# A four-layer graph network on one core: layers 1 and 2 with plain fp32 matmuls, layer norms by statistics instructions and ACT, and the last attention in an order written out by hand

## The chip, the core and the metric

The kernel runs on one core of one Trainium2 chip. A core has five engines, each with its own queue of instructions that it works off in order: PE (TensorE, matmuls; its weight loads are listed as PEld), DVE (VectorE), ACT (ScalarE), POOL (GpSimd, which also issues the indirect DMAs, the gathers) and SP (SyncE, which issues the plain DMAs). They wait for one another through semaphores only. SBUF is the working memory, 128 partitions wide; PSUM takes the matmul results. The metric is the device time of one execution in microseconds (us), the median of several. A profile is one execution recorded by the hardware.

## What is computed

There are 8 batches (B), 2048 nodes (N) and 64 features (D). The graph `adj` is symmetric, has every node's own edge, and about nine neighbours a node. Each layer's output is added to x and layer-normed:

```python
x = _layernorm(x + _L0_gnn_ref(x, adj, ...))   # attention from two scores per node, over neighbours
x = _layernorm(x + _L1_gnn_ref(x, ..., adj))   # per feature: softmax over neighbours of softplus(x*w0+b0)*wa + ba
x = _layernorm(x + _L2_gnn_ref(x, adj, ...))   # relu(x@W_self + b_self + mean over neighbours of x @ W_neigh + b_neigh), own layer norm
x = _layernorm(x + _L3_gnn_ref(x, adj, ...))   # four heads of dot-product attention, Wo, then a second attention on h2:

scores = jnp.einsum('...nd,...md->...nm', h, h)
scores = jnp.where(mask, scores, NEG)
attn = jax.nn.softmax(scores, axis=-1)
return jnp.einsum('...nm,...md->...nd', attn, h) + b
# out2 = _gat_layer(h2, mask, bo);  z2 = leaky_relu(out2, 0.2);  layer norm of z2 with gamma, beta
```

Layers 1 and 2 need sums over all neighbours, for which the kernel multiplies with the whole 2048 x 2048 edge matrix. Layer 0 and the two attentions of layer 3 work on lists of edges.

## The kernel before

**Tiling.** The nodes are cut into NT = 16 tiles of 128 (P), one node a partition; a tile of features is 128 x (8 x 64) = 128 x 512. `X` holds all 16 tiles in SBUF through all layers. The first stage turns `adj` into `ET` (the edge matrix transposed, fp8, 0 or 1), into lists `src` of neighbours, and into 0/1 selections `SelT` and `Sel` that spread node values to edges and add edge values up to nodes. A node tile's edges fill 3 x 4 blocks of 128 edges (GS = 3 steps s, NG = 4 groups g of 32 nodes), and each block's neighbour rows are fetched by one gather on POOL (`gather`, L164).

**Order.** A scheduler orders the instructions of each engine by program order, priorities and free buffers, except inside the four heads of layer 3, where the order of PE, ACT, DVE and POOL is the program's own (`tc.manual_schedule`). Pools (`bufs=n`) hand out n buffers per name in turn; a buffer is written again only when its last reader is done. Pools of a finished stage give their memory to the next stage's.

**Layer norm** (L123 to L141, helper `layer_norm`) takes a group of tiles ("chunks"). Per tile: sum on DVE (L129), times 1/64 (L130), subtraction (L131), square on ACT (L133), sum on DVE (L134); then once per group `inv_sqrt` (L117 to L121, a starting value and three Newton steps, ten short DVE operations), and per tile the multiplication on DVE (L138), and gamma and beta on POOL (L140, L141) where there are any. Layers 0, 1 and 2 norm in groups of four tiles, the second attention tile by tile.

**Layer 1** (L389 to L447). For each tile t it makes R: y = X*w0+b0 (DVE), softplus by Abs, Exp and Ln on ACT, e = y*wa (DVE), r = exp(e) (ACT) and r*y (DVE). Exp and Ln need different tables on ACT, so that tables are loaded in between. The fp32 r is then split into three bf16 pieces whose sum is r: ACT casts (L426, L428), DVE subtracts (L427), POOL makes the last (L429). The matmuls (L436) run over 16 row tiles `it`, 16 tiles jt, three pieces q and two halves h: 1536 matmuls of 128x128 fp8 weights with 512 bf16 columns. DVE divides (L441, L442) and POOL adds to X (L444).

**Layer 2** (L451 to L504). Per tile: transpose X (L107, L108), one fp32 matmul set with W_self and W_neigh (L479), S = own part (L481), and the neighbour part split into three bf16 pieces of Y (L486 to L489). Then 768 matmuls (L494) of ET with Y, scaling and relu (L497, L498), and per four tiles a layer norm of S with gamma and beta, X += S (L503), a layer norm of X.

**Layer 3, heads** (L524 to L740). POOL copies X to a table in memory (`xtab`, L529); 192 gathers of its rows, four heads' scores and sums; `through_wo` adds the heads up to h2 and writes it to `htab` (SP). This part, up to about 2204 us, is PE's.

**Layer 3, second attention** (L741 to L792, scheduler's order). Per tile it loads hi (its own rows of htab) and converts SelT and Sel; then six units (s, pair of groups), each: two gathers of htab rows into hs (POOL), two matmuls pe = selection x hi (L767), pr = pe*hs and its sum sc (DVE, L770, L773), w = exp(sc+shift) (ACT, L775), pr = hs*w (POOL, L776), and per group the matmuls that add pr into po (L780) and w into pd (L782). After the six units: 1/pd, z = po/pd (L784, L786), + bo (L787), leaky relu (L788), layer norm with gamma and beta, + X (L790), layer norm, store (L792).

Of the kernel before, what the change touches and what calls it, by code (L numbers as in the profile page):

```python
# [21 lines left out]
F32 = mybir.dt.float32  # L22
# [26 lines left out]
def kernel(ctx: ExitStack, tc: tile.TileContext, ins: dict, out: bass.AP):  # L49
# [42 lines left out]
    def along(v):  # L92

        return v.unsqueeze(len(v.shape)).to_broadcast([*v.shape, D])
# [27 lines left out]

    def layer_norm(chunks, pool, gamma=None, beta=None):  # L123

        shape = list(chunks[0].shape)
        n = len(chunks)
        mu, var, rstd, tmp = (small.tile([P, n, B], F32, name=f"ln_{k}{n}") for k in "mvrt")
        for c, v in enumerate(chunks):
            nc.vector.tensor_reduce(mu[:, c], v, AX.X, ALU.add)  # L129
            nc.vector.tensor_scalar_mul(mu[:, c], mu[:, c], 1.0 / D)  # L130
            nc.vector.tensor_tensor(v, v, along(mu[:, c]), ALU.subtract)  # L131
            sq = pool.tile(shape, F32, name="sq")
            nc.scalar.activation(sq, v, AF.Square)  # L133
            nc.vector.tensor_reduce(var[:, c], sq, AX.X, ALU.add)  # L134
        nc.vector.tensor_scalar(var, var, 1.0 / D, EPS, op0=ALU.mult, op1=ALU.add)
        inv_sqrt(rstd, var, tmp)
        for c, v in enumerate(chunks):
            nc.vector.tensor_tensor(v, v, along(rstd[:, c]), ALU.mult)  # L138
            if gamma is not None:
                nc.gpsimd.tensor_tensor(v, v, over(gamma, shape), ALU.mult)  # L140
                nc.gpsimd.tensor_tensor(v, v, over(beta, shape), ALU.add)  # L141
# [3 lines left out]
    ET = main.tile([P, NT, N], FP8, name="ET")  # L145
# [14 lines left out]
    for g in range(NG):  # L160
        nc.vector.memset(group[g * GN:(g + 1) * GN, g:g + 1], 1.0)

# [218 lines left out]

# [5 lines left out]
    with ExitStack() as l1:  # L389
        wp = l1.enter_context(tc.tile_pool(name="l1w", bufs=1))  # L390
        wk = l1.enter_context(tc.tile_pool(name="l1k", bufs=2))
        pa = l1.enter_context(tc.tile_pool(name="l1pa", bufs=6, space=PSUM))
# [16 lines left out]
        R = wp.tile([P, NT, 3, 2, 2, HB * D], BF16, name="R")  # L409
        for t in range(NT):  # L410
# [7 lines left out]
            nc.vector.scalar_tensor_tensor(y, y, 0.0, e, op0=ALU.max, op1=ALU.add)  # L418
            nc.vector.tensor_tensor(e.rearrange("p (b d) -> p b d", d=D), y.rearrange("p (b d) -> p b d", d=D),
                                    over(wa, [P, B, D]), ALU.mult)  # L420
            r = wk.tile([P, 2, 2, HB * D], F32, name="r")
            nc.scalar.activation(r[:, :, 0], e.rearrange("p (h n) -> p h n", h=2), AF.Exp)
            nc.vector.tensor_tensor(r[:, :, 1], y.rearrange("p (h n) -> p h n", h=2), r[:, :, 0], ALU.mult)
            rf = r.rearrange("p h a n -> p (h a n)")
            pieces = [R[:, t, q].rearrange("p h a n -> p (h a n)") for q in range(3)]
            nc.scalar.copy(pieces[0], rf)  # L426
            nc.vector.tensor_tensor(rf, rf, pieces[0], ALU.subtract)  # L427
            nc.scalar.copy(pieces[1], rf)  # L428
            nc.gpsimd.tensor_tensor(pieces[2], rf, pieces[1], ALU.subtract)  # L429

        for it in range(NT):
            po = [pa.tile([P, 2, HB * D], F32, name="pa") for _ in range(2)]
            for jt in range(NT):
                for q in range(3):
                    for h in range(2):
                        nc.tensor.matmul(po[h].rearrange("p a f -> p (a f)"), ET[:, jt, it * P:(it + 1) * P],  # L436
                                         R[:, jt, q, h].rearrange("p a f -> p (a f)"),
                                         start=(jt == 0 and q == 0), stop=(jt == NT - 1 and q == 2))
# [921 lines left out]
```

## Time and profile before

| | us |
|---|---|
| three runs | 2860.0, 2861.23, 2864.49; median 2861.23 |
| the profiled execution's own time | 2860.0 |
| its span, first to last instruction | 2858.1 |
| mean granted TensorE clock, 1 being full | 0.795 |

| engine | busy us | share of the span | instructions |
|---|---|---|---|
| PE | 2117.8 | 74% | 11631 |
| DVE | 1642.5 | 57% | 2924 |
| POOL | 1254.1 | 44% | 1015 |
| ACT | 754.7 | 26% | 1180 |

The chain of work that ended last gives PE 41% of the span, POOL 25%, DVE 13%, time with no visible cause ("issue") 12%. The stages in time: the graph and layer 0's preparation to about 240 us, layer 0 to 624, layer 1 to 1009, layer 2 to 1223 and its last norms to about 1250, tables and weights of layer 3 to 1304, heads to 2204, the second attention from 2232. An fp32 matmul stands in the records as two instructions, so that L620's 768 matmuls are 1536 records. An engine that idles while another one sets the pace costs nothing; what a stage waits for last is what counts.

### The profile page before, as it was taken

Reading aid. Unit: us, or ns where it says so; the run is one execution under the profiler, and the core shown is the slowest. Engines: PE = TensorE matmul, PEld = TensorE weight load, DVE = VectorE, ACT = ScalarE, POOL = GpSimd, SP = SyncE. Lnnn points to the kernel's source line nnn. Section 1 sums busy time; section 2 is a strip of 40 time slices with the busy share of each in tenths; the row PEclk is TensorE's granted clock in tenths of the full one; section 3 lists DMA queues with packets and bytes.
Section 4 is the critical chain, followed back from the end, with each engine's and each line's share of the span. In section 5 each row is a group of like instructions: output and inputs, shape, how many; then the busy total and the mean of one; then the engine's idle time right before and its main releaser. Section 6 shows DMA issues by size and latency. Waiting matters only on the chain.

```text
span 2858.1 us, 31030 instructions
## 1 busy us (share of the span) xinstructions
PE 2117.8 (74%) x11631; PEld 1217.2 (43%) x11678; DVE 1642.5 (57%) x2924; ACT 754.7 (26%) x1180; POOL 1254.1 (44%) x1015
## 2 busy tenths in 40 slices
PE   2363333327899989928999999999999678766662
PEld 2362111102344464416777777777777111111110
DVE  7974465655633355764344444444443487888877
ACT  4541111028200040104344444444443111110100
POOL 0037888843200032453223333333231687777773
PEclk9985555559999999959999999999999555555555
DMA  7214544520000000022222221222120334333330
GB/s 206 89 37 129 141 131 139 142 63 1 0 1 0 1 3 1 1 82 77 60 60 74 64 63 60 75 64 65 58 67 27 112 107 114 104 94 98 96 92 16
DMA packets 101264, 200.89 MB, mean 70 GB/s; under 512 B 51953, under 2 KB 51953, under 8 KB 99057
## 3 DMA queue, kind: packets, MB, share of 16 engines
q0 software_dynamic: 46080, 151.82, 18.5%
q1 hardware_dynamic: 38384, 42.79, 4.6%
q10 hardware_dynamic: 16640, 4.20, 0.7%
q8 instruction: 95, 1.56, 0.2%
q14 instruction: 65, 0.52, 0.1%
HBM read 181.91 MB, written 16.84 MB: 70 GB/s over the span
## 4 chain that ended last, share of the span: by engine, by line
PE 41%; POOL 25%; DVE 13%; issue 12%; ACT 4%; DMA 2%; ACTq 1%; SPq 0%; another core or an unknown queue 0%; POOLq 0%; DVEq 0%
PE pscore L620 12%; POOL hs L164 12%; PE pa L436 9%; PE po L640 6%; POOL pr L776 6%; PE pt L612 4%; POOL hs L362 2%; PE pm L666 2%; PE pm L652 2%; PE pm L657 2%; PE pm L598 2%; DVE tops L206 1%; DMA hs<-htab,src 1%; DVE key L195 1%; DVE hs L362 1%
## 5 line engine op out<-in xcount | busy, mean ns | idle before, releaser
L627 DVE SCALAR_TENSOR_TENSOR w<-w,Sel 128x1024 f32<-128x1024 f32 x192 | 235.4, 1226 | 495.8 <-ACT w L624 495.8
L164 POOL DMA_INDIRECT hs<-htab,src x384 | 409.8, 1067 | 113.7 <-issue 80.2
L164 POOL DMA_INDIRECT xs<-xtab,src x192 | 232.6, 1211 | 398.2 <-PE po L640 374.4
L620 PE MATMUL pscore<-U,xsT 128*128 128x256 f32 x1536 | 376.8, 390 | 19.0 <-ACT U L600 19.0
L436 PE MATMUL pa<-R,ET 128*128 128x512 bf16 x1505 | 339.6, 383 | 53.5 <-ACT R L426 30.5
L620 PEld LDWEIGHTS pscore<-U,xsT 128*128 128x128 f32 x1536 | 286.2, 197 | 56.6 <-ACT U L600 23.4
L767 PE MATMUL pe<-hi,selTf 32*128 32x512 f32 x384 | 227.6, 1122 | 50.5 <-DVE pr L770 45.1
L436 PEld LDWEIGHTS <-ET 128*128 128x128 fp8e4 x1536 | 151.1, 99 | 243.2 <-issue 43.3
L624 ACT ACTIVATE w<-pscore 128x1024 f32<-128x1024 f32 x192 | 196.8, 1025 | 187.1 <-PE pscore L620 184.2
L776 POOL TENSOR_TENSOR pr<-hs,w 128x1024 f32<-128x1024 f32 x96 | 187.1, 1949 | 89.4 <-ACT w L775 88.2
L640 PE MATMUL po<-w,xs 128*64 128x128 f32 x3072 | 213.3, 282 | 1.6 <-DVE w L627 1.6
L640 PEld LDWEIGHTS po<-w,xs 128*64 128x64 f32 x3072 | 166.0, 138 | 109.1 <-issue 58.7
L672 POOL TENSOR_TENSOR h<-h,h2h 128x512 f32<-128x512 f32 x48 | 61.0, 1270 | 261.8 <-DVE h2h L668 252.6
L614 ACT COPY xsT<-pt 128x512 f32<-128x512 f32 x192 | 112.6, 586 | 203.7 <-PE pt L612 199.7
L494 PE MATMUL pa<-Y,ET 128*128 128x512 bf16 x752 | 165.1, 379 | 0.8
L770 DVE TENSOR_TENSOR pr<-pe,hs 128x1024 f32<-128x1024 f32 x96 | 116.7, 1219 | 81.5 <-issue 69.8
L352 PE MATMUL pe<-s1g,selTf 128*128 128x32 f32 x96 | 23.2, 400 | 162.2 <-DVE w L354 113.9
L441 DVE RECIPROCAL rec<-pa 128x256 f32<-128x256 f32 x32 | 53.9, 1726 | 144.9 <-PE pa L436 144.3
L133 ACT ACTIVATE sq<-X 128x512 f32<-128x512 f32 x48 | 30.2, 629 | 401.6 <-DVE X L131 377.1
L767 PEld LDWEIGHTS pe<-hi,selTf 32*128 32x128 f32 x384 | 55.9, 302 | 186.6 <-DVE pr L770 69.0
L612 PE MATMUL pt<-ident,xs 128*128 128x128 f32 x768 | 131.5, 295 | 1.6 <-DMA xs<-xtab,src 1.5
L444 POOL TENSOR_TENSOR X<-X,rec 128x256 f32<-128x256 f32 x32 | 22.5, 726 | 239.9 <-DVE rec L442 239.9
(524 smaller groups left out, 3498.5 us busy)
## 6 DMA issues: line engine op xcount, KB each, us to landing
at<-in_adj SPq DMA_DIRECT2D x16, 1024.0 KB
hs<-htab,src POOLq DMA_INDIRECT x384
htab<-H SPq DMA_DIRECT2D x16, 260.0 KB
X<-in_x ACTq DMA_DIRECT2D x16, 256.0 KB
xtab<-Xo SPq DMA_DIRECT2D x16, 256.0 KB
xi<-xtab SPq DMA_DIRECT2D x16, 256.0 KB
htab<-h SPq DMA_DIRECT2D x16, 256.0 KB
hi<-htab SPq DMA_DIRECT2D x16, 256.0 KB
```

Of the source, the lines that this page charges most:

```text
L164: nc.gpsimd.indirect_dma_start(out=dst, out_offset=None, in_=table[:, :], in_offset=bass.IndirectOffsetOnAxis(ap=src[:, it, s, g:g + 1], a ...
L436: nc.tensor.matmul(po[h].rearrange("p a f -> p (a f)"), ET[:, jt, it * P:(it + 1) * P], R[:, jt, q, h].rearrange("p a f -> p (a f)"), star ...
L494: nc.tensor.matmul(po, ET[:, jt, it * P:(it + 1) * P], Y[:, jt, k], start=(jt == 0 and k == 0), stop=(jt == NT - 1 and k == 2))
L612: nc.tensor.transpose(pt[:, p], xss[k][:, p * P:(p + 1) * P], ident)
L614: nc.scalar.copy(xsTs[k], pt)
L620: nc.tensor.matmul(pscore[:, p], xsTs[k][:, p], Us[it % 2][:, p, :, :, g * GN:(g + 1) * GN].rearrange("p k h i -> p (k h) i"), start=True, ...
L624: nc.scalar.activation(w.rearrange("p a h i -> p (a h i)"), pscore.rearrange("p a h i -> p (a h i)"), AF.Exp)
L627: nc.vector.scalar_tensor_tensor(w3, w3, 3.0e38, edge, op0=ALU.min, op1=ALU.mult)
L640: nc.tensor.matmul(po[half, p], xss[k][:, f0:f0 + D], ws[k][:, p, k_ * HN:(k_ + 1) * HN], start=(s == 0 and p == 0), stop=(s == GS - 1 and ...
L767: nc.tensor.matmul(pe[:, k].rearrange("p b d -> p (b d)"), selTf[nodes, s * P:(s + 1) * P], hi[nodes, :], start=True, stop=True)
L770: nc.vector.tensor_tensor(pr.rearrange("p k b d -> p (k b d)"), pe.rearrange("p k b d -> p (k b d)"), hs.rearrange("p k b d -> p (k b d)") ...
L776: nc.gpsimd.tensor_tensor(pr.rearrange("p k b d -> p (k b) d"), hs.rearrange("p k b d -> p (k b) d"), along(w.rearrange("p k b -> p (k b)" ...
```

## The change

Four things are changed together; the parts of the file that serve other graphs are untouched.

- **Layers 1 and 2 in fp32.** R and Y are kept in fp32, without pieces. For each row tile, `edges` converts a column block of ET (128 x 2048) to fp32 on DVE, and the matmuls use it: 512 in layer 1 and 256 in layer 2, each with fp32 weights and 512 fp32 columns. In layer 1 the halves h come one after the other, with four PSUM buffers for six; wa and the product with r move from DVE to POOL.
- **Layer norm** by `bn_stats`: on pairs of batches with features outermost, so that even and odd elements of one instruction are two batches. Mean and variance come from its output; ACT then applies scale and bias, one operation per batch (8 a tile). gamma and beta stay on POOL. Layer 2's gamma, beta and addition now alternate tile by tile.
- **ET's memory** is given back after layer 2.
- **Second attention.** The heads write h2 + bo to a second table, `ktab`, from which the second attention gathers (hi still comes from htab), so that bo is not added later. Its order is written out: unit u+4's gathers, unit u+1's score, unit u+2's pe matmuls, unit u's multiplication (every third on DVE, the rest on POOL) and sums, and the work after a tile spread over the next tile's units.

```diff
+    def norm_stats(chunks):
+        n = len(chunks)
+        st = small.tile([P, n, NP, 6], F32, name=f"st{n}")
+        for c, v in enumerate(chunks):
+            for a in range(NP):
+                nc.vector.bn_stats(st[:, c, a], v[:, 2 * a:2 * a + 2, :].rearrange("p b d -> p d b"))
+        triples = st.rearrange("p n a (k m) -> p (n a k) m", m=3)
+        var, rstd, tmp, nmr = (small.tile([P, n * B], F32, name=f"ln_{k}{n}") for k in "vrtm")
+        nc.vector.tensor_scalar(var, triples[:, :, 2], 1.0 / D, EPS, op0=ALU.mult, op1=ALU.add)
+        inv_sqrt(rstd, var, tmp)
+        nc.vector.scalar_tensor_tensor(nmr, triples[:, :, 1], -1.0, rstd, op0=ALU.mult, op1=ALU.mult)
+        return rstd, nmr
+    def normed(chunks, stats):
...
+                nc.scalar.activation(v[:, b], v[:, b], AF.Identity, scale=rstd[:, k:k + 1], bias=nmr[:, k:k + 1])
...
+    def edges(dst, it):
+        nc.vector.tensor_copy(dst, ET[:, :, it * P:(it + 1) * P])
...
-        R = wp.tile([P, NT, 3, 2, 2, HB * D], BF16, name="R")
+        R = wp.tile([P, NT, 2, 2, HB * D], F32, name="R")
...
-            nc.scalar.copy(pieces[0], rf)
-            nc.vector.tensor_tensor(rf, rf, pieces[0], ALU.subtract)
-            nc.scalar.copy(pieces[1], rf)
-            nc.gpsimd.tensor_tensor(pieces[2], rf, pieces[1], ALU.subtract)
+            nc.gpsimd.tensor_tensor(s, f.rearrange("p h (b d) -> p (h b) d", d=D), over(wa, s.shape), ALU.mult)
+            nc.scalar.activation(R[:, t, :, 0], s.rearrange("p (h b) d -> p h (b d)", h=2), AF.Exp)
+            nc.gpsimd.tensor_tensor(R[:, t, :, 1], f, R[:, t, :, 0], ALU.mult)
         for it in range(NT):
-            po = [pa.tile([P, 2, HB * D], F32, name="pa") for _ in range(2)]
-            for jt in range(NT):
-                for q in range(3):
-                    for h in range(2):
-                        nc.tensor.matmul(po[h].rearrange("p a f -> p (a f)"), ET[:, jt, it * P:(it + 1) * P],
...
+            A = wk.tile([P, NT, P], F32, name="A")
+            edges(A, it)
             for h in range(2):
+                po = pa.tile([P, 2, HB * D], F32, name="pa")
+                pof = po.rearrange("p a f -> p (a f)")
+                for jt in range(NT):
+                    nc.tensor.matmul(pof, A[:, jt], R[:, jt, h].rearrange("p a f -> p (a f)"),
...
+                nc.scalar.copy(Y[:, t, g * 2 * P:(g + 1) * 2 * P].rearrange("p (q n) -> p q n", q=2), py[:, :, 1])
...
+                nc.tensor.matmul(po, A[:, jt], Y[:, jt], start=(jt == 0), stop=(jt == NT - 1))
...
+                    hb = wk.tile([P, B, D], F32, name="hb")
+                    nc.gpsimd.tensor_tensor(hb, h2s[it], over(bo, hb.shape), ALU.add)
+                    nc.sync.dma_start(ktab[it * P:(it + 1) * P, :], hb.rearrange("p b d -> p (b d)"))
...
+            def weigh(u):
+                eng = nc.vector if u % 3 == 1 else nc.gpsimd
+                wxs[u] = fk.tile([P, 2, B, D], F32, name="wx", bufs=3)
+                eng.tensor_tensor(wxs[u].rearrange("p k b d -> p (k b) d"), hss[u].rearrange("p k b d -> p (k b) d"),
+                                  along(ws[u].rearrange("p k b -> p (k b)")), ALU.mult)
+            def add_up(u):
...
+                for k in range(2):
+                    nodes = slice((g + k) * GN, (g + k + 1) * GN)
+                    nc.tensor.matmul(po[nodes], self_[:, s, nodes], wxs[u][:, k].rearrange("p b d -> p (b d)"),
+                                     start=(s == 0), stop=(s == GS - 1))
+                    nc.tensor.matmul(pd[nodes], self_[:, s, nodes], ws[u][:, k], start=(s == 0), stop=(s == GS - 1))
...
+            after = {1: divide, 2: norm, 3: residual, 5: norm, 6: store}
+            PER = GS * NG // 2
+            AHEAD = 4
+            with tc.manual_schedule(engines=engines):
+                for u in range(AHEAD):
+                    fetch(u)
+                expand(0)
+                expand(1)
+                score(0)
+                for u in range(len(units) + PER):
+                    if u + AHEAD < len(units):
+                        fetch(u + AHEAD)
+                    if u + 1 < len(units):
+                        score(u + 1)
+                    if u + 2 < len(units):
+                        expand(u + 2)
+                    if u < len(units):
+                        weigh(u)
+                        add_up(u)
+                    for j, f in after.items():
+                        it, r = divmod(u - j + 1, PER)
+                        if r == 0 and 1 <= it <= NT:
+                            f(it - 1)
```

`fetch`, `score` and `expand` hold the gathers, L770 to L775 and L767 of before; `residual` holds gamma, beta and + X.

## The prediction

> **What bounds the kernel now.** I read the page first (busy shares, slices, costliest groups), then the chain of waits, then the busy time of each engine in stretches that I cut at the first and last start of each stage's main matmul, then the timeline at the seams. The stages follow one another, each with its own limit, so one share for the whole span says little. In the table by stretches the columns are stretch, length, then busy us (x instructions) of PE, PEld, DVE, ACT, POOL, then the granted TensorE clock.
>
> ```profile
> 240.00:624.00 384.00, 130.03 (x564) 51.63 (x564) 200.74 (x286) 37.84 (x75) 308.49 (x224) 0.54 0.49 134
> 624.00:738.00 114.00, 70.26 (x277) 28.72 (x284) 63.61 (x99) 89.15 (x115) 33.70 (x16) 0.89 0.00 1
> 738.00:1009.00 271.00, 269.34 (x1229) 122.41 (x1252) 104.27 (x165) 9.45 (x15) 21.35 (x31) 1.00 0.00 1
> 1009.00:1057.00 48.00, 39.55 (x192) 33.12 (x193) 34.89 (x87) 29.60 (x77) 21.10 (x32) 0.93 0.02 5
> 1057.00:1223.00 166.00, 165.16 (x754) 75.12 (x768) 108.08 (x226) 18.25 (x31) 51.44 (x40) 1.00 0.00 1
> 1304.00:2204.00 900.00, 879.58 (x6628) 693.33 (x6628) 385.95 (x450) 386.32 (x520) 280.22 (x227) 0.98 0.21 62
> 2232.00:2520.00 288.00, 222.16 (x604) 48.22 (x608) 217.90 (x303) 29.56 (x77) 228.62 (x177) 0.51 0.40 115
> 2520.00:2800.00 280.00, 182.84 (x522) 40.35 (x516) 230.18 (x349) 28.91 (x71) 198.87 (x148) 0.51 0.30 89
> ```
>
> Layer 0 (240 to 624) is POOL's: 308 of 384 us, and 0.30 us of unlabelled gap behind each of its 192 gathers. Layer 1's and layer 2's matmuls (738 to 1009, 1057 to 1223) and the four heads (1304 to 2204) are PE's, at over 97%. From 624 to 738 ACT leads, preparing R. The second attention, from 2232, is nobody's alone: POOL, DVE and PE are each 65 to 82% busy and the clock is 0.51. Its groups (operation, shapes, count, busy us and mean ns, idle before):
>
> ```profile
> L164 POOL DMA_INDIRECT hs<-htab,src x192 | 195.9, 1020 | 57.0 <-issue 30.7 <-POOL pr L776 20.7 <-DMA htab<-h 4.6
> L776 POOL TENSOR_TENSOR pr<-hs,w 128x1024 f32<-128x1024 f32 x96 | 187.1, 1949 | 89.4 <-ACT w L775 88.2
> L770 DVE TENSOR_TENSOR pr<-pe,hs 128x1024 f32<-128x1024 f32 x96 | 116.7, 1219 | 81.5 <-issue 69.8 <-PE po L780 11.2
> L121 DVE SCALAR_TENSOR_TENSOR ln_r<-ln_t,ln_r 128x8 f32<-128x8 f32 x96 | 45.1, 480 | 0.6
> L787 DVE TENSOR_TENSOR z<-z,bo 128x512 f32<-128x512 f32 x16 | 27.9, 1745 | 0.2
> ```
>
> The reader should see that POOL is owed 195.9+57.0+187.1+62.3 (three residual operations a tile) = 502 us of the 564 us from the first L776 (2248.0) to the end of the last (2812.1), the rest being waits for w; and that an 8-element DVE operation takes 480 ns on average although the same line takes about 170 when nothing else runs.
>
> **What the Trainium skill says.** "FP8 and Floating Point Precision", TensorE Precision Notes: true fp32 takes four passes. The trace agrees: the 64 fp32 matmuls L657 stand as 128 records of 616 ns, against 379 ns for a one-pass bf16 record of the same 512 columns; 237 ns more is one more pass, so two passes a record. "TensorE: Matmul & The Clock Gate", Part 1: the clock is at half rate until the array is busy; here 1.00 in layers 1 and 2, 0.51 in the second attention even at 77% busy. "GPSIMD Engine Reference", Key points: POOL shares its SBUF interfaces with those VectorE instructions that have two SBUF inputs or run in a 2-port mode. The trace agrees: L121 lasts 1.91 us beside a POOL multiply of 1.90. For ACT, "ScalarE: Activation LUTs", What ACT_TABLE_LOAD costs, charges 93 ns per pointer operand; L309, with two, takes 810 ns against 620 for L415 without, as stated. No page prices bn_stats.
>
> **The change part by part**, against the profiled execution's own 2860.0 us (span 2858.1; the median of three runs, 2861.23, is 1.2 above).
>
> 1. Layer 1's and 2's matmuls. Forty-nine bf16 records end 10.74 us after the first starts: (10.74-0.379)/48 = 0.216 us each. So before: 1536 x 0.216 = 331 us and 768 x 0.216 = 166 us. Eight fp32 records of 256 columns take 1.89 us: (1.89-0.379)/7 = 0.216, two passes of 256; hence 0.43 per 512-column record, 0.86 per matmul. A weight load (190 ns) hides behind 430. After: 512 x 0.86 = 440 and 256 x 0.86 = 220.
>
> 2. How much of layer 1 hides under the preparation of R. Before, PE starts at 638.7 and a pair of node tiles takes ACT 12.8 us. After, per pair, ACT loses four casts (about 1.0 us each) but the built order holds four table loads instead of two: 4 x 1.29 + 2 x (0.57+0.57+0.67+0.58) = 9.9, taken as 10.1. Layer 0's last norm now puts 32 ACT operations of about 0.36 us (384 fixed plus 64 elements, less the overlap) = 11.4 us between the first two tiles' Exp and Ln: I walk R(0) to 643 and the last R to 715, 20 us earlier than 735. But PE's order is fixed: until the last R arrives it has issued 37 matmuls, the two groups of the first row tile and a few of the next, so 475 x 0.86 = 408 us remain, plus 3 for buffers: end at 1126, not 1009. Cost +117 (110 to 126).
>
> 3. Preparation of Y. The removed casts and subtractions lay beside PE, busy 39.6 of 48 us; they give 3 us. Layer 1's last norm: stats 6 us, then 32 ACT operations, 11.4 us, which stand in ACT's queue before all but two of the copies that PE waits for; before, DVE's part delayed one tile. Cost +8 (4 to 14). Layer 2 itself +54. edges(), 2048 elements on DVE (L195, as long, takes 2.3 us), is written one tile ahead, under 13.8 us of matmuls and in layer 1 under 27.5; without that cover it would cost up to 2.3 us on each of 32 tiles. What it cannot hide is one wait when the first two A are given back, in the 3 us of part 2.
>
> 4. Layer 2 to 3. The last group's two norms: stats 2.3+2.7, first normed chunk 2.9, twelve POOL operations 16.5, then POOL's 16 table copies, the first 12 beside the second norm: about 48 us to the last table write against 56. -8 (-18 to +3). ET's freed memory frees nothing sooner, since POOL's copies queue behind the last addition anyway.
>
> 5. Layer 0. Per tile DVE loses two two-input operations (1.4 us) that made POOL wait, and the bn_stats that replace them have one input. If all came back, 22 us; I take -12 (-25 to 0).
>
> 6. Heads: one POOL add (1.3 us) and a table write per tile where POOL is 31% busy: hidden but for the last, +1. The adds and writes stand before the next gathers on POOL and before the next xtab read on SP, both several steps ahead of need; if that lead were gone they would cost 16 x 1.3. They take the place of L787 (1.7 us on DVE). bo's load moves from the second attention's start to the heads' and is waited for only there.
>
> 7. Second attention, per tile of six units. POOL: 12 gathers (195.9+57.0)/16 = 15.8, four multiplies 7.8, three residual operations 3.9: 27.5 us. DVE: six scores 6 x 2.26, two multiplies 2.3, divide 1.5, two norms of 4 bn_stats plus 12 short operations. bn_stats is not in this trace. From reduce (1.21 us for 1024 elements, 0.68 for 512) 128 would last 0.28 us, and the next starts 0.09 earlier: 0.2 is the low end, since every element is read once at least; if it reads twice, 0.45. I take 0.2 (0.45 would cost 2 us of DVE a tile, of which part comes out in the wait below): norm 0.8+2.4. Sum 24, with waits for POOL's multiplies 27. PE at half clock: 2.0 for pe, 1.85 for po, 0.2 for pd, six times: 24.4. So POOL sets it, but in order: the residual waits for norm (DVE) and 8 ACT operations (2.9 us). DVE may start that unit's score only 4.5 us after the multiply of two units before, since PE's expand stands behind the previous add_up; then score, multiply, norm (7 us) and ACT (3.2) end near 15 us of POOL's cycle, and POOL is there at 12. What queues behind it: gathers and the next multiply, for which PE waits. 27.5+3 = 30.5 us a tile (28 to 34) against 35.3. 16 x 30.5 = 488 against 564: -76. Fill -2. Drain: 46 us from the last multiply to the end becomes PE 2.2, divide 1.9, norm 3.5, ACT 3, POOL 4, norm 3.5, ACT 3, store about 3: 24 to 25, -21.
>
> Sum: -12+117+8+54-8+1-76-2-21 = +61, so 2921 us.
>
> **Rivals.** (a) PE takes over the second attention: the new order puts pd between the two po of a unit. Before, the two po stand together and four records end in 1.92 us, overlapped. If pd breaks that, a unit is 5.76 us at clock 0.51, 34.6 a tile: 2921+66 = 2987. For it: strict order in the program. Against: in layer 0 eight po records of four column groups end in 1.93 us, so a group does not wait for another's queue; and a fully busy PE might get its full clock. (b) Faster, one mechanism: fewer two-input DVE operations, so POOL no longer waits at the shared interface, in layer 0 (all 25) and in the second attention, where gathers run at their undisturbed 1.25 and multiplies at 1.90: 15+7.6+3.8 = 26.4 us a tile and no wait for the norm. 2921-13-66 = 2842. It decides only below some 27 us a tile. Against: 24 short two-input operations a tile remain. (c) The fixed order does not do what it says: stalls trade places, 35.3 us a tile remain: 2998.
>
> **How the numbers follow.** Forecast 0.70 (about 2862 to 2975), (a) 0.13, (b) 0.11, (c) 0.06. 0.2% (5.7 us) is about what a measurement of this kernel can tell from no change. The range 2862 to 2988 takes in the forecast's own unknowns and (a) up to its value, and leaves out (b) and (c), 0.17. Of the forecast, 0.05 falls within 0.2%: faster 0.11, same 0.05, slower 0.84.
>
> **What would show it.** fp32 records spaced 0.43 us at clock 1.00, with layer 1's last near 1126 less layer 0's gain; ACT's 32 norm operations in a row near 626 and after layer 1; heads starting about 160 us later; six units every 30.5 us with POOL's waits in front of the residual; some 25 us after the last multiply. Wrong if PE issues more of layer 1 during R, if a unit of PE takes 5.8 us, if bn_stats is far from 0.2 us, or if POOL shows no waits.

## The result, and the profile after

The changed kernel takes 2958.82 us (median of four runs, 2956.77 to 2964.96) against 2860.61 for the kernel before in the same comparison: 1.0345 times as long, 95% interval 1.0326 to 1.0363. So the change costs about 98 us where 61 were forecast: the direction and the range were right, the size was 37 us short. Its profiled execution has a span of 2958.0 us, 99.9 longer than that of before.

The first view is the busy time of each engine by stretches, cut at the seams of the changed kernel: the columns are stretch, length, then busy us (x instructions) of PE, PEld, DVE, ACT, POOL, the granted TensorE clock, the DMA share and GB/s.

```profile
240.00:635.00 395.00, 127.35 (x564) 51.66 (x564) 177.36 (x275) 59.10 (x154) 309.25 (x224) 0.54 0.47 130
635.00:741.00 106.00, 51.50 (x77) 19.42 (x78) 29.98 (x50) 89.41 (x129) 40.78 (x32) 0.72 0.00 0
741.00:1148.00 407.00, 406.88 (x949) 179.80 (x947) 103.64 (x175) 32.13 (x96) 23.45 (x31) 1.00 0.00 0
1148.00:1204.00 56.00, 40.36 (x192) 33.45 (x193) 20.43 (x52) 29.37 (x79) 1.04 (x2) 0.88 0.02 4
1204.00:1424.00 220.00, 220.00 (x514) 97.25 (x512) 73.33 (x226) 65.01 (x194) 48.05 (x36) 1.00 0.00 1
1496.00:2392.00 896.00, 876.86 (x6595) 691.38 (x6596) 384.90 (x449) 385.60 (x519) 299.38 (x242) 0.98 0.22 67
2424.00:2925.00 501.00, 372.17 (x1128) 101.43 (x1128) 417.35 (x730) 119.78 (x356) 367.60 (x298) 0.50 0.41 116
```

The reader should see three things. Layer 1's and layer 2's matmuls (third and fifth line) leave PE no idle time at the full clock and are simply longer: 407 and 220 us. DVE lost work in layer 0 (177 us busy for 205), yet that stretch did not become shorter. And in the second attention (last line) DVE is now the busiest engine, 83% of the stretch, ahead of PE (74%) and POOL (73%).

From its page, the matmul groups of layers 1 and 2 (line, engine, operation, tiles, shapes, count, busy us and mean ns, idle before and what ended it): two records a matmul, and in layer 2 no idle time at all.

```profile
L445 PE MATMUL pa<-R,A 128*128 128x512 f32 x1024 | 458.4, 610 | 61.9 <-POOL R L436 61.9
...
L497 PE MATMUL pa<-Y,A 128*128 128x512 f32 x512 | 219.9, 592 | 0.0
```

Of the groups of its second attention, in the same columns, these matter:

```profile
L176 POOL DMA_INDIRECT hs<-ktab,src x192 | 193.7, 1009 | 53.4 <-issue 44.8 <-DMA ktab<-hb 4.2 <-POOL wx L805 2.5
L805 POOL TENSOR_TENSOR wx<-hs,w 128x1024 f32<-128x1024 f32 x64 | 123.8, 1935 | 2.7 <-ACT w L800 1.5
L795 DVE TENSOR_TENSOR pr<-pe,hs 128x1024 f32<-128x1024 f32 x96 | 117.1, 1220 | 66.1 <-PE pe L790 55.5 <-issue 10.6
...
L133 DVE TENSOR_SCALAR ln_v<-st 128x8 f32<-128x8 f32 x32 | 56.2, 1757 | 1.1
...
L130 DVE BATCH_NORM_STATS2 st<-z 128x6 f32<-128x128 f32 x128 | 27.9, 281 | 6.8 <-POOL z L832 6.8
L830 POOL TENSOR_TENSOR z<-z,g 128x512 f32<-128x512 f32 x16 | 20.3, 1268 | 87.6 <-ACT z L143 87.6
```

POOL's wait for w, 88 us before, is gone; in its place it stands 87.6 us in front of the residual, 5.1 us on nearly every tile. An operation on eight numbers (L133) lasts 1757 ns on average: it is held while POOL multiplies, as L121 was before.

Where the time went is best read from the seams between the stages, each the first start of one operation or the end of a stage's last matmul. The table gives the length of each stage in us, from the profiled executions of the two kernels and of four experiments that are told below.

| stage | before | after | x_fp32 | x_norms | x_fixed | x_bf16 |
|---|---|---|---|---|---|---|
| to layer 1's first y | 628.1 | 635.5 | 627.8 | 639.5 | 628.4 | 635.7 |
| to layer 1's last matmul | 380.6 | 512.4 | 504.2 | 391.7 | 380.6 | 391.8 |
| Y | 48.5 | 56.3 | 48.8 | 59.1 | 48.3 | 59.1 |
| layer 2's matmuls | 165.9 | 219.9 | 240.8 | 165.9 | 166.0 | 165.9 |
| to the heads' first score | 81.0 | 72.2 | 71.6 | 69.4 | 78.7 | 69.3 |
| heads, to shift | 926.2 | 923.8 | 924.0 | 924.8 | 924.8 | 925.1 |
| second attention, to the end | 627.8 | 537.9 | 629.2 | 626.6 | 536.1 | 536.7 |
| span | 2858.1 | 2958.0 | 3046.4 | 2877.0 | 2762.9 | 2783.6 |

Layer 1 and layer 2 lose 132 and 54 us, layer 0 and Y another 7 and 8; the second attention gives back 90, the end of layer 2 nine and the heads two.

### The profile page after: what moved, and what is told of

Its sections match the earlier page's. It is cut to its first block, busy times and chain, and to the rows that moved or that the text cites. A ratio compares the mean times of both kernels' runs of the same rounds, so it can differ in the third digit from the quotient of the medians.

```text
span 2958.0 us, 29903 instructions
## 1 busy us (share of the span) xinstructions
PE 2247.2 (76%) x10910; PEld 1296.4 (44%) x10910; DVE 1466.8 (50%) x2844; ACT 929.3 (31%) x1802; POOL 1192.9 (40%) x983
## 4 chain that ended last, share of the span: by engine, by line
PE 56%; POOL 15%; DVE 14%; ACT 6%; issue 5%; DMA 2%; ACTq 1%; SPq 0%; POOLq 0%; DVEq 0%
PE pa L445 13%; PE pscore L626 12%; PE pa L497 7%; POOL hs L176 7%; PE po L646 6%; PE pt L618 4%; PE pe L790 2%; POOL hs L374 2%; PE pm L672 2%; PE po L813 2%; PE pm L658 2%; PE pm L663 2%; DMA hs<-htab,src 2%; PE pm L604 1%; DVE pr L795 1%
## 5 line engine op out<-in xcount | busy, mean ns | idle before, releaser
L445 PE MATMUL pa<-R,A 128*128 128x512 f32 x1024 | 458.4, 610 | 61.9 <-POOL R L436 61.9
L445 PEld LDWEIGHTS pa<-R,A 128*128 128x128 f32 x1024 | 199.2, 196 | 321.6 <-issue 243.0
L143 ACT ACTIVATE X<-X,ln_m,ln_r 128x64 f32<-128x64 f32 x384 | 128.5, 426 | 372.4 <-DVE ln_m L135 372.3
L176 POOL DMA_INDIRECT hs<-htab,src x192 | 219.8, 1145 | 56.7 <-issue 50.1
L497 PE MATMUL pa<-Y,A 128*128 128x512 f32 x512 | 219.9, 592 | 0.0
L176 POOL DMA_INDIRECT hs<-ktab,src x192 | 193.7, 1009 | 53.4 <-issue 44.8
L790 PE MATMUL pe<-hi,selTf 32*128 32x512 f32 x384 | 197.4, 1136 | 15.3 <-DVE pr L795 9.4
L497 PEld LDWEIGHTS pa<-Y,A 128*128 128x128 f32 x512 | 97.3, 190 | 122.0 <-issue 121.3
L143 ACT ACTIVATE z<-z,ln_m,ln_r 128x64 f32<-128x64 f32 x256 | 88.3, 426 | 170.7 <-DVE ln_m L135 164.6
```

The source lines that it names most:

```text
L143: nc.scalar.activation(v[:, b], v[:, b], AF.Identity, scale=rstd[:, k:k + 1], bias=nmr[:, k:k + 1])
L176: nc.gpsimd.indirect_dma_start(out=dst, out_offset=None, in_=table[:, :], in_offset=bass.IndirectOffsetOnAxis(ap=src[:, it, s, g:g + 1], a ...
L445: nc.tensor.matmul(pof, A[:, jt], R[:, jt, h].rearrange("p a f -> p (a f)"), start=(jt == 0), stop=(jt == NT - 1))
L497: nc.tensor.matmul(po, A[:, jt], Y[:, jt], start=(jt == 0), stop=(jt == NT - 1))
L790: nc.tensor.matmul(pe[:, k].rearrange("p b d -> p (b d)"), selTf[nodes, s * P:(s + 1) * P], hi[nodes, :], start=True, stop=True)
```

## The experiments

### One part at a time

Four kernels separate the change. **x_bf16** is the changed kernel with layers 1 and 2 taken back:

```diff
-        R = wp.tile([P, NT, 2, 2, HB * D], F32, name="R")
+        R = wp.tile([P, NT, 3, 2, 2, HB * D], BF16, name="R")
...
-        Y = wp.tile([P, NT, BD], F32, name="Y")
+        Y = wp.tile([P, NT, 3, BD], BF16, name="Y")
```

> Layers 1 and 2 compute in three bf16 pieces as before; the new norms and the new second attention stay. Theory F (fp32 is the whole loss: its matmuls, and the end of layer 1's cover under the preparation of R): the other parts keep what the seams of the two traces show, layer 0 +7, the 32 norm operations on ACT in front of R +11, Y +8, tail -9, heads -2, second attention -90, so about 2860-75 = 2785 us. Theory N (the norms cost more than the seams show, since the fp32 loops hid part of their waits): 2800 to 2820. If bf16 were no faster here than fp32, 2958.

**x_fp32** puts only those two layers, with edges(), into the kernel before:

```diff
-        R = wp.tile([P, NT, 3, 2, 2, HB * D], BF16, name="R")
+        R = wp.tile([P, NT, 2, 2, HB * D], F32, name="R")
...
+            edges(A, it)
```

> The kernel before with layers 1 and 2 in fp32 alone. Theory F: last R near 728 (a pair of node tiles every 11.7 us, no norm operations between), then 475 matmuls of 0.86 us, so layer 1 ends near 1137 instead of 1008, layer 2 +54, Y -3: about 2860+180 = 3040 us. If the loops alone counted (440+220 against 331+166), 3023. If the fp32 parts and the norms share a loss, below 3023.

**x_norms** puts only the new norms of layers 0, 1 and 2 into it:

```diff
+    def layer_norm(chunks, pool, gamma=None, beta=None):
+        normed(chunks, norm_stats(chunks))
...
-                layer_norm([z], fk, g3, b3)
+                old_norm([z], fk, g3, b3)
```

> The kernel before with the new norms in layers 0, 1 and 2 alone; the second attention keeps the old norm. Theory N: +15 to +35, 2875 to 2895, with layer 0 about 7 us longer and POOL's waits ahead of its big multiply near 20 us instead of 4. Theory of the prediction (fewer two-input DVE operations free POOL): -12 in layer 0, then +11 at R, +8 at Y, -8 at the tail: 2859.

**x_fixed** puts in only the second attention in its fixed order, with ktab and its own norms:

```diff
+                    nc.gpsimd.tensor_tensor(hb, h2s[it], over(bo, hb.shape), ALU.add)
...
+            with tc.manual_schedule(engines=engines):
+                for u in range(AHEAD):
+                    fetch(u)
```

> The kernel before with the fixed second attention and its gathered bias alone. All theories: 2860-92 = 2768, since nothing of the other parts reaches it; a tile every 31.9 us with 5.1 us of POOL's wait in front of the residual. Above 2780 would say that the earlier parts helped it.

Measured: x_bf16 0.9767 (0.9751 to 0.9783), 2785.96 us; x_fp32 1.0672 (1.0654 to 1.0690), 3045.27; x_norms 1.0084 (1.0067 to 1.0101), 2877.52; x_fixed 0.9698 (0.9682 to 0.9714), 2766.06; the kernel before 2852.13 beside them. What follows: the fp32 layers are the whole loss and more, the new norms in the first three layers cost rather than help, and the fixed second attention alone is a gain of 3.0%. The expectations were reckoned from 2860, and the kernel before took 2852 beside these four, so the differences are what can be compared: x_bf16 -66 us where theory F had -75, x_fp32 +193 for +180, x_norms +25 for +15 to +35, x_fixed -86 for -92. All four bear out the theory named, but x_fp32 came near its number in part by luck: in its trace layer 2 lost 75 us instead of 54, and the end of layer 2 gave 9 us back that nobody had counted.

By stages, the three single parts sum to +112 us of span for +99.9 of the whole change. The ratios sum to +4.5% instead of +3.45%; the kernel before took from 2852 to 2861 us in the different comparisons, and that enters three times into such a sum, so the stages are the better ledger. In it two entries of the parts do not simply add. The end of layer 2 becomes 9 to 12 us shorter either by the fp32 layers or by the norms, and no more by both. About half of it is DVE's lag: in the kernel before DVE begins the last scaling of layer 2 4.6 us after PE's end (1227.7 against 1223.1), in x_fp32 and in x_norms at once. And layer 2 in fp32 takes 240.8 us beside the old norms but 219.9 beside the new. The matmul group there in x_fp32, over layer 2's stretch alone, to be set beside L497 of the changed kernel above, which has 219.9 us and no wait:

```profile
L492 PE MATMUL pa<-Y,A 128*128 128x512 f32 x512 | 226.3, 605 | 14.6 <-DVE A L391 14.6
```

Beside the old norms PE waited three times, 4.8 to 4.9 us each, for the cast of edges(); the first time (1268) the cast stood in DVE's queue among the operations of the old norms and began 30 us after the one before it (1266.9 after 1236.6). The longer records, 605 ns on average for 592, make up the other 6 us. Beside the new norms no wait is left.

The third part of the change, ET's memory given back after layer 2, was not tried alone. It is in x_bf16 and x_fixed and not in x_fp32 and x_norms; in x_fixed the stretch that it could reach, from layer 2 to the heads, takes 78.7 us instead of 81.0, so that it is worth 2 us at most there.

### Layer 0: whose are the 7 us?

The prediction gave layer 0 a gain of 12 us and it lost 7.4. The built order of POOL's queue suggests why. POOL's instructions of layer 0 in the changed kernel, in the last group of four tiles (timeline; start, duration, engine, line, operation, and in brackets the idle time before it and who ended it):

```profile
575.18 0.94 POOL L176 DMA_INDIRECT hs<-htab,src  x1 [0.30 <-issue]
576.43 0.95 POOL L176 DMA_INDIRECT hs<-htab,src  x1 [0.30 <-issue]
577.39 3.63 POOL L374 TENSOR_TENSOR hs<-hs,w 128x2048 f32<-128x2048 f32 x1
581.18 0.98 POOL L176 DMA_INDIRECT hs<-htab,src  x1 [0.16 <-issue]
586.50 5.72 POOL L374 TENSOR_TENSOR hs<-hs,w 128x2048 f32<-128x2048 f32 x1 [4.33 <-DVE st L130]
592.37 2.86 POOL L176 DMA_INDIRECT hs<-htab,src  x1
```

Two big multiplies of successive tiles have one gather between them, and it is the last that the second needs. It is issued at 581.18, w is there at 586.4, and POOL stands still for 4.33 us; in the order of before, z's addition and mostly five gathers of the next tile lie between a tile's last gather and its multiply. (The release is put down to a bn_stats; the operations that end just before are those on w, which waited for the gathered rows.) This occurs once in each of the last three groups of four. Two kernels test it.

**y_l0old** is the changed kernel with layer 0's norm as before:

```diff
             if it % 4 == 3:
-                layer_norm([X[:, t] for t in range(it - 3, it + 1)], wk)
+                old_norm([X[:, t] for t in range(it - 3, it + 1)], wk)
```

> The changed kernel with layer 0's norm as before. Theory O (the new norm changes the order of POOL's queue in layer 0: in three groups of four tiles two big multiplies stand with one gather between, and POOL waits 4.3 us for that gather; and its 32 ACT operations stand in front of R): layer 0 ends 7 to 11 us earlier, the last R another 11, so 2958 - 20 = 2938 us, ratio near 1.027. Rival (layer 0's 7 us come from elsewhere): R alone, -11, 1.031.

**z_l0order** keeps the new norm and only holds POOL's queue to the order of before:

```diff
+        with tc.manual_schedule(engines={mybir.EngineType.Pool}):
+            fetch0(0, 0, 12)
+            fetch0(1, 0, 5)
...
+                fetch0(it + 1, 5, 12)
                 den = wk.tile([P, NG, B], F32, name="den")
...
+                fetch0(it + 2, 0, 5)
                 if it % 4 == 3:
```

> The changed kernel with POOL's queue in layer 0 fixed to the order that it had before: five gathers of the next tile ahead of each big multiply, seven behind it, then z. The norm stays the new one. Theory O (the order alone cost layer 0's 7 us): first y near 628 as before, ratio 1.032. The prediction's own step (fewer two-input DVE operations free POOL): y near 616, 1.028. Rival (the norm's operations themselves): y at 635, 1.0345.

Measured: y_l0old 1.0287 (1.0271 to 1.0302), z_l0order 1.0285 (1.0268 to 1.0302). Layer 1's y, whose first start marks the end of layer 0 (minimum, median, maximum ns; first to last start), in the changed kernel, in y_l0old and in z_l0order:

```profile
L425 DVE TENSOR_SCALAR y<-X,w,bb x16: 537/1014/1594, 635.5 to 722.5; 128x512 f32<-128x512 f32 x16
```

```profile
L446 DVE TENSOR_SCALAR y<-X,w,bb x16: 540/1014/1592, 628.7 to 705.1; 128x512 f32<-128x512 f32 x16
```

```profile
L437 DVE TENSOR_SCALAR y<-X,w,bb x16: 537/1014/1594, 620.4 to 707.6; 128x512 f32<-128x512 f32 x16
```

By this mark the new norm, with its order held, ends layer 0 7.7 us sooner than the kernel before (628.1) and 15.1 sooner than in the changed kernel. The mark flatters it: the new norm's scaling of the last group, 32 operations on ACT, comes after the first y, the old norm's on DVE before it. The last addition to X in layer 0 (start and duration on DVE), in the kernel before, the changed kernel and z_l0order, is free of that:

```profile
619.25 0.69 DVE L378 SCALAR_TENSOR_TENSOR X<-z,e 128x512 f32<-128x512 f32 x1
```

```profile
631.30 0.69 DVE L390 SCALAR_TENSOR_TENSOR X<-z,e 128x512 f32<-128x512 f32 x1
```

```profile
616.22 0.69 DVE L401 SCALAR_TENSOR_TENSOR X<-z,e 128x512 f32<-128x512 f32 x1
```

The order still costs 15.1 us, but of the gain only 3.0 are left. This gain is known to a few us only: in the other kernels with the old norm in layer 0 and the scheduler's order the same addition starts between 619.5 and 622.8. POOL was freed a little: its 16 big multiplies take 74.1 us in the kernel before, 70.1 in the changed one and 67.7 in z_l0order. The waits of POOL's multiply show the order's part, first in the kernel before, then in the changed kernel, then in z_l0order (waits over layer 0; total us, times, longest):

```profile
POOL z L374 <- DVE z L373: 9.0, 1, 9.0
POOL hs L362 <- ACT w L356: 4.0, 1, 4.0
```

```profile
POOL hs L374 <- DVE st L130: 12.9, 3, 4.3
POOL z L386 <- DVE z L385: 6.4, 1, 6.4
POOL hs L374 <- ACT w L368: 5.1, 1, 5.1
```

```profile
POOL z L397 <- DVE z L396: 6.8, 1, 6.8
POOL hs L384 <- ACT w L378: 3.8, 1, 3.8
```

So the order is the cause of the loss, as theory O has it; its other half, that the norm as such is neutral, is not what the first y says, which at 620.4 is nearer to the prediction's 616 than to 628. By the last addition the operations gain a quarter of the 12 us forecast, and the scheduler's new order, which came with them and is gone in y_l0old, takes 15. The written order with the old norm throughout was not run, so that a small part of the gain may be that order's own. y_l0old shows the second cost of the norm: from the first y to the start of the last R product it takes 92.5 us (628.7 to 721.2) against 103.1 (635.5 to 738.6), 10.6 us less, and the 32 operations of the last group's norm last 10.7 in the changed kernel. In z_l0order that stretch takes 103.3 as well. In the whole the two come out equal, 1.0287 and 1.0285: what the new norm gains in layer 0 by the first y it gives back in front of R.

### Layer 1's preparation of R

ACT's groups from 638 us to the last R in the changed kernel:

```profile
L430 ACT ACT_TABLE_LOAD x15 | 19.2, 1283 | 0.3
...
L143 ACT ACTIVATE X<-X,ln_m,ln_r 128x64 f32<-128x64 f32 x32 | 10.7, 426 | 0.1
L435 ACT ACT_TABLE_LOAD x8 | 10.3, 1283 | 0.1
L435 ACT ACTIVATE R<-s 128x512 f32<-128x512 f32 x16 | 10.1, 629 | 12.0 <-POOL s L434 11.9
...
L429 ACT ACT_TABLE_LOAD x7 | 9.0, 1283 | 0.1
```

Thirty table loads, 38.5 us, and 12 us of waiting for s, which the change moved from DVE (0.68 us, L419 before) to POOL (1.27 us). The kernel before had 16 loads, and a wait of the same size at this place, for DVE's product with wa (its group in the same columns, from 628 to 735 us):

```profile
L422 ACT ACT_TABLE_LOAD x8 | 10.3, 1283 | 11.9 <-DVE e L419 11.9
```

**y_sdve** moves s back:

```diff
-            nc.gpsimd.tensor_tensor(s, f.rearrange("p h (b d) -> p (h b) d", d=D), over(wa, s.shape), ALU.mult)
+            nc.vector.tensor_tensor(s, f.rearrange("p h (b d) -> p (h b) d", d=D), over(wa, s.shape), ALU.mult)
```

> The changed kernel with the product s of layer 1's preparation on DVE instead of POOL. Theory: ACT waits 1.4 us a pair of node tiles for POOL's s (1.27 us there, 0.68 on DVE, and behind R's product in POOL's queue); without it a pair takes 10.3 instead of 11.7, and the last R comes 11 us sooner, with 37 matmuls issued before it as now: ratio 1.031, about 2947. Rival (ACT is full anyway): unchanged, 1.0345.

Measured 1.0256 (1.0241 to 1.0272), more than was expected. The same groups in y_sdve:

```profile
L430 ACT ACT_TABLE_LOAD x8 | 10.3, 1283 | 0.1
L435 ACT ACT_TABLE_LOAD x8 | 10.3, 1283 | 0.1
...
L435 ACT ACTIVATE R<-s 128x512 f32<-128x512 f32 x16 | 9.9, 630 | 0.9
```

The wait is gone, as the theory has it; but 14 of the 30 table loads went as well (18 us), since with s on DVE the built order keeps the pair of node tiles together through Exp, Ln and Exp. The last R is ready at 717.4 instead of 739.9 and layer 1 ends at 1117.5 instead of 1147.9; the 8 us between these two gains are matmuls that PE had already issued when the last R came (400 us remain instead of 408). The theory named the place and missed the larger half of it. One edit changed both the wait and the loads, so their shares are read from the trace and were not tested apart. The Trainium skill, "ScalarE: Activation LUTs", What ACT_TABLE_LOAD costs, gives about 1283 ns a load and a drain of 1380 ns on top. The load agrees, every one here takes 1283 ns. The drain is not seen: in the changed kernel a load starts at 649.56 and the Ln behind it at 650.86, so 1.30 us is the whole price, and 14 loads are 18 us.

### The second attention: POOL's wait or DVE's work?

The prediction took POOL's order as the limit, with a wait in front of the residual. **y_later** changes x_fixed so that POOL finds the norm done:

```diff
-            after = {1: divide, 2: norm, 3: residual, 5: norm, 6: store}
+            after = {1: divide, 3: norm, 5: residual, 6: norm, 7: store}
```

> The kernel with only the second attention fixed (2766 us beside 2852 before), and in its order each step after a tile's units moved: the first norm one unit later, after the next score; the residual two units later; the second norm and the store one unit later. Theory W (POOL's order is the bound, and its 5.1 us of wait in front of each residual is lost time): the wait goes, and 31.9 us a tile becomes 27.5 to 29, so 2766 - 16 x 3.7 = 2707 us (2700 to 2725). Rival D (DVE and PE are as late as POOL, so the wait trades places): over 2750.

Measured 0.9706 (0.9691 to 0.9721): no gain over x_fixed's 0.9698. Waits over the second attention, in x_fixed (its residual is L836 too):

```profile
POOL z L836 <- ACT z L143: 76.8, 15, 5.1
...
POOL wx L811 <- ACT w L806: 1.6, 1, 1.6
...
PE pe L796 <- ACT selTf L771: 1.4, 1, 1.4
```

and in y_later:

```profile
PE pe L796 <- ACT selTf L771: 55.3, 15, 4.0
...
POOL wx L811 <- ACT w L806: 33.0, 14, 4.9
POOL z L836 <- ACT z L143: 32.8, 14, 2.5
```

The wait went down from 76.8 to 32.8 us, and 33 us for w and 55 us of PE's for the converted edge list came up: rival D. DVE's busy share shows what they have in common (440 us of x_fixed, then 440 us of y_later, columns as above):

```profile
2260.00:2700.00 440.00, 330.47 (x1000) 90.05 (x1000) 375.05 (x670) 110.34 (x328) 323.22 (x262) 0.50 0.41 115
```

```profile
2260.00:2700.00 440.00, 331.19 (x1000) 89.68 (x1000) 399.35 (x659) 105.95 (x319) 337.65 (x264) 0.50 0.40 116
```

DVE goes from 85% to 91% busy with fewer instructions (659 for 670): its operations on eight numbers L119 and L121 last 0.55 us on average instead of 0.17, its multiply 1.44 instead of 1.22, and L133 0.47 instead of 1.92. So other operations than before are held while POOL multiplies, and together for longer. If DVE is the limit, less of its work must help. **z_pair** takes the statistics of two tiles at once, which halves the number of short operations:

```diff
-            def norm(it):
-                normed([zs[it]], norm_stats([zs[it]]))
+            def stats_of(it):
+                held["s"] = norm_stats([zs[it], zs[it + 1]])
...
+            after = [(2, stats_of), (2, lambda it: scaled(it, 0)), (3, lambda it: scaled(it, 1)),
+                     (4, residual), (7, lambda it: residual(it + 1)),
+                     (8, stats_of), (8, lambda it: scaled(it, 0)), (9, lambda it: scaled(it, 1)),
+                     (9, store), (10, lambda it: store(it + 1))]
```

> The kernel with only the second attention fixed (ratio 0.970), with its two norms taken for two node tiles at once: the same 8 statistics and 16 ACT operations a norm, but 12 short DVE operations for two tiles instead of 24, and the tile's two casts one unit earlier; the residuals in the units in which DVE, not POOL, multiplies. Theory V (DVE with its waits for the shared interface is what a tile of 31.9 us takes, POOL's wait being only its shadow): 24 short operations of 0.20 us a pair, 2.4 us a tile, fall away: 29.5 us, 16 x 2.4 = 38 less, ratio 0.956. Theory W (POOL's order): POOL is owed 26.8 us, 0.942. Rival (PE's ring of expand and add_up at 4.3 us a unit plus its waits): under 10 us, 0.967 to 0.970.

Measured 0.9538 (0.9522 to 0.9554), 2728.14 us. The 96 scores stand in x_fixed and in z_pair at:

```profile
L801 DVE TENSOR_TENSOR pr<-pe,hs x96: 1214/1224/1226, 2236.7 to 2730.0; 128x1024 f32<-128x1024 f32 x96
```

```profile
L799 DVE TENSOR_TENSOR pr<-pe,hs x96: 1209/1223/1226, 2240.4 to 2689.3; 128x1024 f32<-128x1024 f32 x96
```

A tile is six scores: (2730.0 - 2236.7)/95 x 6 = 31.2 us, then 28.4. Theory V expected 2.4 us less and it is 2.8; theory W's 0.942 and the 0.967 of PE's ring lie well outside the interval. But DVE's busy time a tile falls by 1.6 us only, from 26.5 to 24.9 (340.2 of 400 us in x_fixed and 350.7 in z_pair, 2260 to 2660 us), less than the tile does. The edit also moved the casts and the residuals, so that part of the gain may be theirs; y_later, which moved steps alone, gained nothing. In z_pair DVE, POOL and PE are 88, 86 and 85% busy. That a version with less work on DVE is shorter is shown; that DVE alone is the bound is not.

### Towards a version that beats both

**y_best** adds to y_later the new norms in layer 2 alone.

```diff
-                layer_norm([X[:, t] for t in ts], wk)
+                new_norm([X[:, t] for t in ts], wk)
```

> Layers 0 and 1 as before, layer 2 in bf16 pieces as before but with the new norms, whose last group is nearer to the tables of layer 3, and the fixed second attention with the later steps. From the parts: y_later less 9 to 11 at the tail of layer 2: about 2697 us, ratio 0.945. If DVE's freed time in layer 2 gives nothing at the tail, as y_later.

Measured 0.9676 (0.9663 to 0.9690), 0.3% under y_later: the end of layer 2 became 8 us shorter, the rest of its expectation fell with y_later's. **z_best** adds layer 2's norms and one more edit to z_pair:

```diff
-            nc.scalar.copy(pieces[0], rf)
+            nc.vector.tensor_copy(pieces[0], rf)
```

> The paired norms of the second attention, layer 2's norms new (tail 9 us shorter), and in layer 1's preparation the first cast of R on DVE instead of ACT: ACT leads there with 12.8 us a pair, two casts of 1.04 us less make about 2 us a pair, with DVE at 57 of 107 us busy, 8 x 1.5 = 12 sooner. From the parts under theory V: 0.956 - 0.003 - 0.004 = 0.949. If DVE becomes the bound of the preparation, no gain from the cast, 0.953.

Measured 0.9569 (0.9553 to 0.9585), slower than z_pair's 0.9538 although layer 2's end is 11 us shorter. ACT's other cast of R and its tables now wait for DVE (groups of the preparation, z_best):

```profile
L461 ACT CAST R<-r 128x1024 bf16<-128x1024 f32 x16 | 16.7, 1045 | 26.6 <-DVE r L460 25.9
...
L455 ACT ACT_TABLE_LOAD x7 | 9.0, 1283 | 10.0 <-DVE e L452 10.0
```

The last piece of R starts at 753.9 instead of 734.6 in z_pair. The expectation missed: 16 us of ACT's work are saved, but in place of two waits for DVE of 2 and 12 us in the kernel before there are these of 26 and 10 and a third, of 8, for y. **z_last** leaves the cast where it was and takes layer 0's fixed order, with the new norm for three groups and the old one for the last:

```diff
+                    (new_norm if it < NT - 1 else layer_norm)([X[:, t] for t in range(it - 3, it + 1)], wk)
```

> The fixed second attention with paired norms (ratio 0.954), without the cast on DVE; POOL's queue in layer 0 fixed to its order of before, with the new norm for its first three groups of four tiles and the old one for the last, so that no norm operations of ACT stand in front of R; layer 2's norms new. From the parts: layer 0 about 8 us sooner (y at 620 against 628), the tail of layer 2 about 9 shorter: 0.9538 - 17/2859 = 0.948. If the old norm of the last group gives back layer 0's gain, 0.951.

Measured 2716.95 us (2710.84 to 2719.62) against 2860.43, ratio 0.9504 (0.9491 to 0.9517): the fastest here, 5% under the kernel before. It was expected at 0.948, or 0.951 if the old norm of the last group took back layer 0's gain, and lies nearer the second: its first y is at 624.1, four of the eight us hoped for.

## Why the prediction was right, and where it was off

**Layers 1 and 2's matmuls: right.** From the last R (739.9) to the end of layer 1 (1147.9) are 408 us, the number in part 2, and layer 2 takes 219.9 for 220 forecast. x_fp32 shows that this part alone costs more than the whole change.

**The preparation of R: under-priced, and started from the wrong end of layer 0.** With layer 0's gain the prediction stood at 616 for the first y, 631 for the first R and 703 for the last. The trace has 635.5, 656.7 and 739.9. Of these 37 us, 19.4 are layer 0's; 6 stand before the first R, and 11 in the seven pairs of tiles after it, 11.7 us each instead of 10.1. The step that failed is "taken as 10.1": it sums what keeps ACT busy in a pair, the four table loads among it, and no wait. ACT waits 1.5 us a pair for POOL's s, 12.0 in all, and as long a wait, 11.9 us for DVE's product, stood at this place in the trace of before. In y_sdve that wait is gone, and with it 14 of the loads, which had been counted but not traced to the move of s. Three us allowed for buffers were not needed, which leaves layer 1's end 33.9 us late.

**Layer 0: the step that failed.** -12 became +7.4. The prediction's mechanism, fewer two-input operations that make POOL wait, is there but small: POOL's big multiplies take 6.4 us less in z_l0order, and layer 0's last addition comes 3.0 sooner, so that 12 was too much even with the order held; the -7.7 of the first y hold in part work that was put off. What turned the sign is that the prediction priced POOL's instructions in the order of before, where the built order of the changed kernel has three pairs of multiplies almost in a row. It looked at the built order for ACT and PE, and not for POOL, the engine that it had itself named as this stage's limit.

**Y and the end of layer 2: right in number; heads: small.** +7.8 for +8 and -8.8 for -8; the heads gave 2.4 us where 1 was to be lost, and no run says why. For Y the parts fit as well: the norms cost 10.6 us in x_norms, and taking back the casts is worth 2.8 (59.1 in x_bf16, 56.3 in the changed kernel). At the end of layer 2 the number is partly luck: the norms alone shorten it by 11.6, as the prediction has it, but so do the fp32 layers alone, by 9.4, which it does not have.

**Second attention: right in kind, 9 us short in size.** -89.9 for -99. From the first multiply (2438.8) to the end of the last (2932.0) are 493 us instead of 564, so -71 for -76; the drain is 26 us for 46, as forecast; the fill is 18.7 for 17.7, where 2 less were forecast. A tile's z comes every 31.94 us in the middle of the stage, not 30.5, and the wait at the residual is 5.1, not 3: that wait is the term that was too small, for POOL's own share came out at 26.8 where 27.5 were owed. The forecast sum for DVE, 27 us with its waits, was near, 83% of 31.94 being 26.6. That POOL's order with this wait sets the pace is the part that did not hold: in y_later 44 us of the wait went and the tile stayed as long, while z_pair, with fewer operations on DVE, shortened it. The wait was foretold rightly, but it was not what held the stage.

**The rivals.** (a) fell: PE shows the four records of the two po in 1.93 us with pd behind them, and where it need not wait a unit follows the last one after 3.93 us, 23.6 a tile. (b) fell by its own point: 31.9 us a tile are above the 27 from which it decides, and layer 0 gave nothing back. (c) fell: stalls did trade places, at 31.9 and not at 35.3. In total, 33.9 up to the end of layer 1 and 9 in the second attention, less 3 in the heads and 1 elsewhere, are the 39 us by which the spans differ from the forecast.

## What to carry to other kernels

Where a scheduler orders the queues, an edit that only shortens work on one engine can reorder another: read the built order of the engine that bounds the stage before pricing its relief, and if the order matters, write it down. A stage's length is not the sum of what keeps its engine busy: count the waits that its trace already has. A wait is worth its length only if its engine sets the pace; where several engines go round in a ring, here 73 to 85% busy, moving steps only moved the waits, and the version with less work on the fullest one was the shorter. And of a change in several parts run each alone: here one part of -3.0% was buried under one of +6.7%.

## What had not been expected of the hardware

bn_stats of 128 elements lasts 272 to 296 ns and four in a row 0.87 us, so the low end of the estimate, 0.2 us each, was right. A DVE operation with one input is held by POOL's multiply as well as those with two: L133, eight numbers, takes 1.96 us beside the multiply and 0.17 us free of it, 1757 ns on average over its 32 executions in the second attention, 56 us in all, while the two-input operations that follow it, once the multiply is over, take 0.17. The Trainium skill, "GPSIMD Engine Reference", Key points, names such a second class, DVE instructions in a 2-port mode; that L133 runs in one is an inference from its being held, and no run here separates it. And the TensorE clock stays at 0.50 in z_pair's second attention from 2240 to 2660 us with PE busy 351 of these 420 us, whereas 0.98 is granted in the heads, where PE is busy 98% (877 of 896 us).
